# fc2's two upper products taken for both rows of a group together, in seven inner products each

## The chip, the cores and the metric

The kernel runs on one core of one Trainium2 chip, in one launch. The metric is the device time of that launch in microseconds (us). All arithmetic is float32; one matmul of a 128 x 128 weight tile with 256 columns appears in the profile as two records.

## The reference, cut to what matters

There are 16 rows b, each an x of 512 tokens by 512 features. A first layer computes h = gelu(x @ fc1.T + fc1_b), 2048 wide. A second layer, fc2, gives 384 shared outputs, and the row's own expert gives the last 128; so each row has its own 512 x 2048 weight matrix, of which three quarters are common to all rows. Then

```python
x = x + concat(h @ fc2.T + fc2_b, h @ experts_w[idx[b]].T + experts_b[idx[b]])      # x1
s = tanh(x @ W1 + b1) @ v                                 # one score per token
p = softmax(where(mask(prompt_type), s, -1e30))           # prefix, postfix or all but itself
x = x + (p @ x) / count
```

The last three lines are called pooling here. The kernel does them with a running maximum and linear recurrences along the tokens.

## The kernel before

The 16 rows go in 8 groups of two rows (`i`, `b0 = 2 * i`). A group has two stages on TensorE: fc1 for both rows at once, then fc2 for one row after the other.

Both layers use Strassen's scheme in Winograd's form: a product of 2 x 2 blocks takes seven block products and some sums. fc1 does so twice over: seven outer products, each of seven inner ones, 128 weight rows deep (`class Outer`, L555; its additions on VectorE are at L604, L618, L629, L645). fc2 does it once (`fc2`, L687): products 1 and 2 (banks `ba`, `bb`; weights `up`, blocks a11 and a12 of the upper half of the weights, which are the same for every row) and products 5, 7, 6, 3, 4 with the lower weights (`lo`) and the row's expert. Each of the seven is 16 matmuls of 256 columns (L724). The moving blocks b11, b12, b21, b22 are quarters of `hT`, the gelu of fc1; their sums (`t1` at L739, then L740, L744, L747) are VectorE's. `x1T` gets the result with the residual `xr` added (L764 to L775).

Weights come through a ring of ten 256 KB tiles, loaded on SyncE's queue in the order of `Ring.plan` and each waiting until the tile ten before it is free. fc1's inputs (`Moving`, tag `xT`) and the output stores use that queue too. PSUM has three banks `bx`, three `by` and one `bd`.

Each engine executes its instructions in the order in which the program issues them. Pooling is a Python generator per row (`class Pooling`, L834): a chain of some 40 small VectorE instructions on the scores (`weights`, L948), a store of the coefficients to DRAM and a load that spreads them over 128 partitions (L1078 to L1083) and ScalarE's copy of them (L1086), then per quarter of `x1T` a multiplication, a scan, two ScalarE passes, a multiplication and an addition (`apply`, L1092), and for most rows four transposes (L1193), each with its four stores (L1198). Every `yield` tells what a step costs VectorE in us by the author's estimate, or, if negative, asks for a pause. The estimates of one pooling add up to 24.15. While the matmuls of the other work are issued, `slot(budget, passed)` spends a small budget on the oldest unfinished pooling; the budgets stand in `SPARE` (fc1, 22.5 in a group's sum) and `SPARE_2` (fc2: 22.9 in a first row, 13.0 in a second). A row's pooling starts in the middle of the next stage: that of a first row in its group's second row, that of a second row in fc1 of the next group. Before a group's fc2 stands `drain(1)` (L1292), after its first row `drain()` (L1351):

```python
    def slot(budget, passed):                       # L1210
        while pools and pools[0].done:
            pools.pop(0)
        if pools:
            pools[0].slot(budget, passed)

    def drain(left=0):                              # L1216
        while len(pools) > left:
            slot(1e9, 1e9)
```

With a budget of 1e9 a pooling's own `slot` (L898) ignores pauses and goes to its end.

Of the kernel before, what the change touches and what calls it, by code (L numbers as in the profile page):

```python
# [9 lines left out]
F32 = mybir.dt.float32  # L10
I32 = mybir.dt.int32
AF = mybir.ActivationFunctionType
ALU = mybir.AluOpType
# [4 lines left out]
def tile_cond_experts_then_prompt_pool(  # L18
# [53 lines left out]
    LOWER = ("s1", "s3", "s2", "s4", "a22")  # L72


    WHERE = (
        (((0, 0), None, False),),
        (((1, 0), (0, 0), False),),
# [5 lines left out]
    )  # L83
    w1s = {
        (o, n): dram.tile([P, PW], F32, name=f"w1s_{o}_{n}") for o in OUTER for n in INNER if not (o in RAW and n in RAW)
    }
    w2s = {(n, h): dram.tile([P, PW], F32, name=f"w2s_{n}_{h}") for n in LOWER[:4] for h in range(2)}

# [4 lines left out]
    def piece1(o, n):  # L93
        (R, C), (r, c) = rc(o), rc(n)
        return fc1T[:, 2 * C + c, ds(R * (HID // 2) + r * PW, PW)]
# [68 lines left out]
    class Ring:  # L164
        def __init__(self):
            self.plan, self.tiles = [], {}
            for i in range(B // 2):
                b = 2 * i
                for o in OUTER:
                    self.plan += [("f1", i, o, p) for p in (INNER if i else INNER_0)]  # L170
                for r in range(2):
                    self.plan += [("up", b + r, "a11", h) for h in range(4)]
                    if not r:
                        self.plan += [("ex", b, "a11", h) for h in range(2)]
                    self.plan += [("up", b + r, "a12", h) for h in range(4)]
                    self.plan += [("ex", b + r, "a12", h) for h in range(2)]
                    self.plan += [("lo", b + r, n, h) for n in LOWER for h in range(2)]
                    if not r:
                        self.plan += [("ex", b + 1, "a11", h) for h in range(2)]
            self.at = 0  # L180
            self.taken, self.free = [], set()
# [14 lines left out]
        def pump(self):  # L196
            while self.at < len(self.plan) and self.room():
                key = self.plan[self.at]
                kind, b, n, h = key
                if kind == "lo" and n not in lower_done:  # L200
                    return
                if kind == "f1" and b == 0:
                    if not start_piece(n, h):
                        return
                else:
                    t = self.tiles[key] = self.tile(key)
                    if kind == "f1":
                        nc.sync.dma_start(t, w1s[n, h] if (n, h) in w1s else piece1(n, h))
                    elif kind == "up":
                        k = rc(n)[1] * KH + 2 * h  # L210
                        nc.sync.dma_start(as_chunks(t, 2), fc2T[:, k : k + 2, : 2 * P])
                    elif kind == "lo" and n in LOWER[:4]:
                        nc.sync.dma_start(t, w2s[n, h])
                    else:
                        nc.sync.dma_start(as_chunks(t), half2(n, 1 if kind == "ex" else 2, h))
                self.at += 1
# [202 lines left out]
            ring.pump()  # L419

    lower_done = {"a22"}

    ring = Ring()

# [262 lines left out]
    def fc2(b, hT, ex, at):  # L687
# [80 lines left out]
        at("3")  # L768
        add(out_block(0, 1), bc, u12, ALU.add)
        if b + 1 < B:  # L770
            xr_next[:] = [residual(b + 1, 0, 0), residual(b + 1, 1, 1)]
        if b + 1 < B:
            product(bd, of("a22"), b21, KH, "4", add=True)
            at("4")
# [47 lines left out]

        nc.scalar.activation(p1.tile([1, 1], F32, tag="c_none", name="none"), ones[0:1, :1], AF.Exp)
        return psc, x1T

# [388 lines left out]
# [3 lines that stand above are left out]
# [6 lines left out]
        "6m": 3.0, "6": 0.4, "3m": 3.0, "3": 2.5, "4m": 2.0,  # L1225
    }

    LAST_2 = {n + q: 1.7 for n in "57633" for q in ("a", "m", "c", "")}
    LAST_2.update({"6": 0.4, "3a": 0.8, "3m": 0.8})
    pool = xi_after = None  # L1230
    for i in range(B // 2):
# [9 lines left out]
        for n in range(7):  # L1241
            before, op = op, Outer(i, n, x, xi, hT)
            if i == 0:
                if n == 2:
                    nc.gpsimd.dma_start(w1_sb, w1)
                elif n == 4:
                    for h in range(2):
                        experts.load(h)
                    lower = Lower()
            for k in range(14):  # L1250
                if k % 2 == 0:
                    op.step(0, STEPS[k // 2])
                elif k >= LAG:
                    op.step(1, STEPS[(k - LAG) // 2])
                elif before:
                    before.step(1, STEPS[(k - LAG) // 2 + 7])
                tick()
                if n == 0 and i:
                    xi = xi_second
                elif n < 6:  # L1260
                    if k == 4:
                        x.outer_sum(n + 1, nc.gpsimd)
                    elif k == 7:
                        xi = x.inner_sums(n + 1, nc.gpsimd, (0, 1))
                    elif k == 10:
                        x.inner_sums(n + 1, nc.gpsimd, (2, 3))
                if i == 0:
                    if (n, k) == (2, 6):
                        start_outer("s4")
                    work()  # L1270
                    if n == 4:
                        lower.load()
                if pool and n == 0:
                    if k == 6:
                        pool.project()
                    elif k == 11:
                        pool.score()
                        pools.append(pool)

                if n or k >= 8:  # L1280
                    slot(SPARE[n], 0.86)
# [4 lines left out]
        if i == 0:  # L1286
# [3 lines left out]
            flush_stores()  # L1290
            xr_next[:] = [residual(0, 0, 0), residual(0, 1, 1)]
        drain(1)  # L1292
        for row in range(2):
            b = b0 + row
            more = row == 1 and b + 1 < B
# [2 lines left out]
            def at(name):  # L1298
                if b == 0:
                    for n in {"1a": ("s1",), "1c": ("s3",), "2m": ("s2",), "2": ("s4",)}.get(name, ()):  # L1300
                        lower.sums(n)
                    if name == "5":
                        fill()
                if row == 0:
                    if name == "1m":
                        for h in range(2):
                            experts.sum1(h)
                        for h in range(2):
                            experts.sums("a11", h)
                    elif name == "2m":  # L1310
                        for h in range(2):
                            experts.sums("a12", h)
                    elif name == "7":
                        nxt["ex"] = Expert(b + 1)
                        for h in range(2):
                            nxt["ex"].load(h)
                    elif name == "3m":
                        for h in range(2):
                            nxt["ex"].sum1(h)
                    elif name == "4m":  # L1320
                        for h in range(2):
                            nxt["ex"].sums("a11", h)
                else:
                    if name == "1a":
                        pool.project()
                    elif name == "1m":
                        pool.score()
                        pools.append(pool)
                    elif name == "2m":
                        for h in range(2):  # L1330
                            experts.sums("a12", h, nc.vector if b + 1 < B else nc.gpsimd)
                    if more and name == "2":
                        nxt["x"] = Moving(i + 1)
                    elif more and name == "7m":
                        nxt["xi"] = nxt["x"].inner_sums(0, nc.vector)
                        nxt["x"].outer_sum(1, nc.vector)
                    elif more and name == "6m":
                        nxt["xi_2"] = nxt["x"].inner_sums(1, nc.vector)
                if b + 1 == B:
                    if name == "1b":  # L1340
                        pool.rush()
                    elif name == "2":
                        before_last.flip_all("xT")
                    elif name == "end":
                        pool.flip_all("tx")
                    elif name in LAST_2:
                        slot(LAST_2[name], 1.7)
                elif name in SPARE_2 and not (row and name in ("3", "4m")):
                    slot(SPARE_2[name] * (0.4 if row and name in ("7m", "6m", "3m") else 1), 3.4)
                if b + 1 == B and name == "3":  # L1350
                    drain()  # L1351

# [53 lines left out]
```

## Time and profile before

| | us |
|---|---|
| time, median of 3 runs (1604.40 to 1608.44) | 1607.59 |
| time of the profiled execution | 1605.61 |
| its span | 1603.8 |
| TensorE busy in the span | 1564.2 |
| VectorE / ScalarE / GpSimd busy | 1160.1 / 621.2 / 393.3 |
| a group in the middle: fc1, 596.6 to 689.2 | 92.6 |
| the fc2 of both its rows, 689.2 to 789.6 and on to 790.5 | 101.3 |

In the profile PE is TensorE, PEld its weight loads, DVE VectorE, ACT ScalarE, POOL GpSimd and SP SyncE; "SPq" and "ACTq" are the issues of DMAs on those queues. A line of a timeline reads: start, duration, engine, line of the kernel, operation, what it writes and reads, how many, and in brackets how long the engine sat idle before it and what ended that. The profiled execution lies 1.98 us under the median, and 1.8 us of it lie outside the span.

### The profile page before, as it was taken

What the parts mean: (1) busy time and instruction counts of PE and PEld (TensorE: products, weight loads), DVE (VectorE), ACT (ScalarE), POOL (GpSimd) and SP (SyncE); (2) the same over time, 40 slices, a digit from 0 to 9 for tenths busy, and PEclk for the clock granted to TensorE, in tenths of its full rate; (3) what the DMA queues carried; (4) which work ended last, traced back from release to release, by engine and by line L of the source; (5) the groups of instructions that cost most, each with busy time, mean ns of one, the idle gap of its engine ahead of it and who ended that gap; (6) DMA issues with size and microseconds to landing.
All of it is one profiled execution on the core that took longest, in us unless ns stands there. A gap on an engine that the chain in (4) does not pass through costs nothing. (4 is left out here: it accounts for less than half of the span.)

```text
span 1603.8 us, 21941 instructions
## 1 busy us (share of the span) xinstructions
PE 1564.2 (98%) x6986; PEld 1317.9 (82%) x6986; DVE 1160.1 (72%) x2108; ACT 621.2 (39%) x1244; POOL 393.3 (25%) x426
## 2 busy tenths in 40 slices
PE   7999999999999999999999999999999999999995
PEld 6788878888788887888888887888878888788884
DVE  7875657967677676777678775887757967668676
ACT  2350145522453324633246223462244521454333
POOL 5541015200360004500045000630016200251020
PEclk9999999999999999999999999999999999999998
DMA  7667646658476574666656675576746658466542
GB/s 252 219 210 231 194 134 165 196 153 252 125 176 189 147 250 125 177 199 166 201 145 177 204 202 159 148 181 189 225 147 164 189 165 251 123 166 187 160 99 53
DMA packets 340094, 284.54 MB, mean 177 GB/s; under 512 B 145292, under 2 KB 264140, under 8 KB 339980
## 3 DMA queue, kind: packets, MB, share of 16 engines
q1 hardware_dynamic: 313580, 244.23, 53.3%
q0 software_dynamic: 5760, 19.97, 3.8%
q10 hardware_dynamic: 20640, 18.94, 3.8%
q8 instruction: 56, 0.92, 0.2%
q14 instruction: 58, 0.48, 0.1%
HBM read 253.55 MB, written 29.45 MB: 176 GB/s over the span
## 5 line engine op out<-in xcount | busy, mean ns | idle before, releaser
L591 ACT ACTIVATE hT<-hT,fc1b_sb 128x256 f32<-128x256 f32 x416 | 179.7, 498 | 64.7 <-DVE hT L645 49.4
L632 POOL TENSOR_TENSOR q<-p,hT 128x512 f32<-128x512 f32 x80 | 106.1, 1327 | 371.7 <-ACT p L625 360.1
L574 PE MATMUL bx<-xi,w_f_s_s 128*128 128x256 f32 x512 | 128.8, 384 | 3.8 <-DVE by L629 2.0
L724 PE MATMUL ba<-hT,w_up_a 128*128 128x256 f32 x512 | 116.7, 381 | 0.0
L724 PEld LDWEIGHTS ba<-hT,w_up_a 128*128 128x128 f32 x512 | 96.5, 190 | 23.1 <-issue 10.7
L574 PEld LDWEIGHTS bx<-xi,w_f_s_s 128*128 128x128 f32 x512 | 96.5, 191 | 22.1 <-DVE ba L618 5.3
L724 PE MATMUL bb<-hT,w_up_a 128*128 128x256 f32 x512 | 113.1, 379 | 0.0
L724 PE MATMUL bd<-hT,e 128*128 128x256 f32 x496 | 112.1, 379 | 0.0
L724 PEld LDWEIGHTS bb<-hT,w_up_a 128*128 128x128 f32 x512 | 97.3, 190 | 13.2
L724 PEld LDWEIGHTS bd<-hT,e 128*128 128x128 f32 x496 | 94.2, 190 | 12.8
L464 POOL DMA_INDIRECT e<-in_expT,rows x32 | 34.6, 1082 | 279.8 <-PE bd L724 241.7
L604 DVE TENSOR_TENSOR hT<-bx,hT 128x512 f32<-128x512 f32 x112 | 75.3, 684 | 32.1 <-PE bx L574 31.9
L574 PE MATMUL bx<-xi,w_f_a_s 128*128 128x256 f32 x384 | 95.9, 383 | 0.7 <-DVE by L629 0.4
L625 ACT COPY p<-bd 128x512 f32<-128x512 f32 x112 | 65.5, 585 | 79.8 <-PE bd L574 78.0
L1086 ACT COPY cb<-cb 128x1024 f32<-128x1024 f32 x15 | 15.7, 1045 | 204.8 <-DMA cb<-co_d 106.6
L629 DVE TENSOR_TENSOR by<-bx,p 128x512 f32<-128x512 f32 x112 | 77.5, 692 | 24.1 <-PE bx L574 23.6
L1151 ACT ACTIVATE v<-f,U,cb 128x512 f32<-128x512 f32 x60 | 48.9, 815 | 108.7 <-DVE U L1126 103.4
L1125 DVE TENSOR_TENSOR_SCAN f<-cb,u 128x512 f32<-128x512 f32 x60 | 79.6, 1326 | 12.9 <-ACT u L1117 12.2
L680 ACT ACTIVATE xr<-xr,fc2b_sb 128x256 f32<-128x256 f32 x96 | 44.9, 500 | 108.4 <-DVE p1x L743 39.2
L1133 DVE TENSOR_TENSOR f<-v,cb 128x512 f32 x60 | 45.9, 765 | 54.0 <-ACT v L1152 53.8
L1193 DVE STREAM_TRANSPOSE yo<-x1T 128x512 f32<-128x512 f32 x60 | 41.2, 701 | 59.2 <-DMA out_y<-yo 56.7
L574 PEld LDWEIGHTS bx<-xi,w_f_a_s 128*128 128x128 f32 x384 | 73.1, 191 | 12.1 <-issue 1.3
(292 smaller groups left out, 3492.7 us busy)
## 6 DMA issues: line engine op xcount, KB each, us to landing
w_up_a<-in_fc2T SPq DMA_DIRECT2D x128, 256.0 KB
w_lo_s<-w2s_s SPq DMA_DIRECT2D x128, 256.0 KB
w_f_s_s<-w1s_s_s SPq DMA_DIRECT2D x112, 256.0 KB
w_f_a_s<-w1s_a_s SPq DMA_DIRECT2D x84, 256.0 KB
w_f_s_a<-w1s_s_a SPq DMA_DIRECT2D x84, 256.0 KB
w_f_a_a<-in_fc1T SPq DMA_DIRECT2D x69, 256.0 KB
w_ex_a<-in_fc2T SPq DMA_DIRECT2D x64, 256.0 KB
xr<-in_xT ACTq DMA_DIRECT2D x64, 256.0 KB
```

What stands on the lines that cost most here:

```text
L574: nc.tensor.matmul(to.rearrange("p (b s) -> p b s", b=2) if len(mv.shape) == 3 else to, w[:, ts(2 * mh + m, P)], mv, start=(not add and m ...
L591: nc.scalar.activation(to[:, m], src[:, m], AF.Gelu, bias=fc1b_sb[:, hc + m : hc + m + 1])
L604: eng.tensor_tensor(to, src, self.place(prev, r, c, mh)[1], ALU.add)
L625: nc.scalar.copy(u["p5"], bd)
L629: add(u["y"], u["x"], u["p5"], ALU.add)
L632: nc.gpsimd.tensor_tensor(self.both(u["q"]), self.both(u["p5"]), self.place(self.to[0][1], 1, 1, mh)[1], ALU.add)
L680: nc.scalar.activation(t[:, m, :], t[:, m, :], AF.Identity, bias=bias)
L724: nc.tensor.matmul(bank[:, m, :], w(m, k), mv[:, k, :], start=(not add and m == 0 and k == 0), stop=(k == depth - 1), skip_group_check=True,)
L1125: V.tensor_tensor_scan(f[dc], c0, turned(u[dc]), 0.0, ALU.mult, ALU.add)
L1133: V.tensor_tensor(f[dc], turned(v[dc]), beta, ALU.mult)
L1151: nc.scalar.activation(v[dc][:, :S], f[dc], AF.Identity, bias=U[:, dc : dc + 1], scale=fac)
L1193: nc.vector.transpose(yo, self.x1T[:, dc, :])
```

## The change

In groups 1 to 6 (`joint`) products 1 and 2 of fc2 are taken for both rows together, each as seven inner products, in the order 1, 5, 6, 2, 7, 3, 4. One inner product is 4 matmuls, of 128 columns of each row. The sums of weights that this needs are made once, in group 0 (`UpperSums`), and kept in DRAM (`w2u`). The sums of `h` are GpSimd's, eight of 128 x 1024 in a group; the banks are combined by VectorE and ScalarE. Products 5, 7, 6, 3, 4 of each row follow (`Joint.row`). The pooling budgets of these groups are new (`JOINT_0`, `JOINT_1`, and four slots of 1.0 in `at_upper`), and add up to 16.9 before the end of the first row and 6.3 in the second. The load of the next group's `xT` is issued in product 5 of the second row; since the new sums lie in the buffer `xT`, it waits for the last read of them, the ScalarE copy behind that product. In group 0, one slot of the second row moves from "3m" to "4a". The diff, cut:

```diff
+    UPPER = ("a11", "s1", "s2", "a12", "s3", "s4", "a22")
+    UP_STEPS = (1, 5, 6, 2, 7, 3, 4)
+    def joint(i):
+        return 0 < i < B // 2 - 1
...
+                if joint(i):          # Ring.plan
+                    u = [("u2", b, o, n) for o in ("a11", "a12") for n in UPPER]
+                    self.plan += u[:4] + ex(0, "a11") + u[4:10] + ex(0, "a12") + u[10:] + lo(0, LOWER)
+                    self.plan += ex(1, "a11") + lo(1, LOWER[:1]) + ex(1, "a12") + lo(1, LOWER[1:])
+                    continue
...
+    class UpperSums:
+        def __init__(self):
+            self.t = p1.tile([P, 8, PW], F32, tag="xT", name="st_upper")
+        def load(self, o):
+            for k, n in enumerate(BLOCKS):
+                nc.scalar.dma_start(as_chunks(self.t[:, k]), half2(o, *rc(n)))
+        def sums(self, o, n):
...
+            nc.vector.tensor_tensor(to, self.t[:, at[in0]], self.t[:, at[in1]], op)
+            nc.gpsimd.dma_start(w2u[o, n], to)
...
+    class Joint:
+        def __init__(self, b0, hT):
+            self.t = p1.tile([P, 4, KH // 2, 2, Q], F32, tag="xT", name=f"th_{b0}")
+            self.o11 = self.t[:, 3]...
+        def sum(self, o, k, eng=nc.gpsimd):
...
+            eng.tensor_tensor(T(k), in0, in1, ALU.subtract)
+        def upper(self, xr, at):
...
+                for p in UP_STEPS:
+                    if p == 1:
+                        u["a"] = bank("by", f"ua_{b0}_{o}")
+                        product(x, 1)
+                        if one:
+                            nc.scalar.copy(u["a"][:, 0, :], x[:, 0, :])
+                        else:
+                            V.tensor_tensor(rows(u["a"]), rows(x), o11(0, 0), ALU.add)
+                    elif p == 5:
+                        product(bp, 5)
+                        nc.scalar.copy(u["p5"][:, 0, :], bp[:, 0, :])
+                        if one:
+                            self.sum("a12", 0)
+                    elif p == 6:
+                        product(x, 6, add=True)
+                        V.tensor_tensor(u["y"][:, 0, :], x[:, 0, :], u["p5"][:, 0, :], ALU.add)
...
+                        self.sum(o, 3)
+                    elif p == 2:
+                        product(u["a"], 2, add=True)
...
+                    elif p == 7:
+                        product(x, 7, add=True)
...
+                    at(f"u{tick}")
...
+        def row(self, r, ba, ex, xr, at, xr_after):
+            bc, bd = (bank("by", f"{n}2_{b}") for n in ("bc", "bd"))
+            product(bc, "s1", self.t1, "5")
+            nc.scalar.copy(out_block(0, 0), self.o11[:, r])
...
+    JOINT_0 = {"5m": 1.0, "5": 2.0, "7m": 1.0, "7": 2.0, "6m": 2.5, "6": 0.4, "3a": 1.0, "3m": 1.0, "3": 2.0}
+    JOINT_1 = {"5": 1.0, "7m": 0.6, "7": 2.5, "6m": 0.6, "6": 0.4, "4a": 1.2}
...
         drain(1)
+        if joint(i):
+            joined.sum("a11", 2)
+            def at_upper(name):
+                if name == "u1":
+                    joined.outer(0, 0)        # t1 of the first row, VectorE
...
+                if name in ("u8", "u9", "u11", "u12"):
+                    slot(1.0, 1.7)
...
+            ba = joined.upper([t() for t in xr_next], at_upper)
+            for r in range(2):
+                x1T = joined.row(...)
+                if r == 0:
+                    experts = nxt["ex"]
+                    drain()
+                before_last, pool = pool, Pooling(b0 + r, x1T)
+            continue
...
+                        nxt["up"] = UpperSums()          # group 0, first row, at "5"
+                        nxt["up"].load("a11")
...
-                elif name in SPARE_2 and not (row and name in ("3", "4m")):
-                    slot(SPARE_2[name] * (0.4 if row and name in ("7m", "6m", "3m") else 1), 3.4)
+                elif row and name == "4a":
+                    slot(SPARE_2["3m"] * 0.4, 5.1)
+                elif name in SPARE_2 and not (row and name in ("3m", "3", "4m")):
+                    slot(SPARE_2[name] * (0.4 if row and name in ("7m", "6m") else 1), 3.4)
```

## The prediction

> **What bounds the kernel now.** I read the page's first part, the waits of TensorE, then the timelines of one group. TensorE is the bound.
>
> ```profile
> PE 1564.2 (98%) x6986; PEld 1317.9 (82%) x6986; DVE 1160.1 (72%) x2108; ACT 621.2 (39%) x1244; POOL 393.3 (25%) x426
> ```
>
> In the middle groups it waits for almost nothing. The largest wait there is at the start of fc1, for the single bank `bd` that product 3 of fc2 has just filled; in the list of waits (total us, times, longest):
>
> ```profile
> PE bd L574 <- DVE x1T L769: 3.5, 3, 1.5
> ```
>
> In TensorE's timeline fc2's products 1 and 2 follow fc1 at once, and start 6.90 us apart: 16 matmuls, so 0.431 us each. The third line is the one long wait near the end: after 2.64 us of idling, 8 matmuls (16 records) took 5.41 us, 1.8 us more than the 3.62 of such a line elsewhere.
>
> ```profile
> 689.24 7.07 PE L724 MATMUL ba<-hT,w_up_a 128*128 128x256 f32 x32
> 696.14 7.07 PE L724 MATMUL bb<-hT,w_up_a 128*128 128x256 f32 x32
> ...
> 1558.40 5.41 PE L805 MATMUL bd<-hT,w_lo_a 128*128 128x256 f32 x16 [2.64 <-DVE p L756]
> ```
>
> So matmuls taken away count in full, as long as no other engine is made late. That is where the change has to be examined.
>
> **What it takes away.** Products 1 and 2 of two rows are 64 matmuls of 256 columns; in seven inner products they are 2 x 7 x 4 = 56. Six groups save 48 x 0.431 = 20.7 us. The banks `bc` and `bd` of fc2 are now both `by`, so fc1 no longer waits for L769: 3.5 us more.
>
> **What moves: the drain ahead of fc2.** The decisive point stands in the order of the changed program, which is fixed when it is built. A first row's pooling gets 6.3 of budget in the second row (13.0 before), then fc1's 22.5, less what the pauses waste. Before, its last transpose is issued within outer product 5 of fc1. In the changed order of groups 2 to 7 all four of its transposes come behind fc1's last addition: `drain(1)` finds this pooling unfinished. The loop then runs until one pooling is left in the list. But a finished pooling is taken from the list only by the next call of `slot`, and that call, with a budget of 1e9, goes on to drive the second one to its end. So VectorE's order reads: last addition of fc1, four transposes of row b0-2, the whole pooling of row b0-1, and only then `outer(0, 0)` and the addition `u["y"]` that inner product 7 waits for. ScalarE has the same: that pooling's passes stand ahead of the copy of inner product 1, which product 6 waits for. On SyncE the stores of eight transposes and the coefficients' round trip stand ahead of the ring loads that follow. TensorE can run 2 x 1.73 = 3.5 us before it needs ScalarE, and 4 x 1.73 = 6.9 us before it needs VectorE.
>
> The length of this burst, from the end of fc1's last matmul (689.24 in the group shown):
>
> First, the last addition of fc1 ends 0.9 after it. Then the transposes of row b0-2. Their buffer `yo` has two places, but one holds the next row's scores, so each waits for the store of the one before: starts 4.75 apart here, 4.75 to 5.45 in other groups (some are held by other work between); 4.9 taken. With no scores in the way the four took 7.3 (743.52 to 750.82).
>
> ```profile
> 664.22 0.71 DVE L1193 STREAM_TRANSPOSE yo<-x1T 128x512 f32<-128x512 f32 x1 [1.72 <-DMA out_y<-yo]
> 668.97 0.71 DVE L1193 STREAM_TRANSPOSE yo<-x1T 128x512 f32<-128x512 f32 x1 [0.60 <-DMA out_y<-yo]
> 689.44 0.69 DVE L604 TENSOR_TENSOR hT<-bx,hT 128x512 f32<-128x512 f32 x1
> 743.52 1.30 DVE L1193 STREAM_TRANSPOSE yo<-x1T 128x512 f32<-128x512 f32 x2 [0.40 <-POOL x1T L1177]
> 747.98 0.71 DVE L1193 STREAM_TRANSPOSE yo<-x1T 128x512 f32<-128x512 f32 x1 [3.15 <-DMA out_y<-yo]
> 750.11 0.71 DVE L1193 STREAM_TRANSPOSE yo<-x1T 128x512 f32<-128x512 f32 x1 [1.42 <-DMA out_y<-yo]
> ```
>
> 3 x 4.9 + 0.7 = 15.4: done at 16.3. Then the chain on the scores. The last group of the kernel before runs it without pauses for row 14, in 9.0 between these two lines and 0.2 for the instruction ahead: done at 25.5.
>
> ```profile
> 1521.57 0.22 DVE L970 SCALAR_TENSOR_TENSOR s<-s,is,s 32x16 f32<-32x16 f32 x1 [1.05 <-DMA s<-srow]
> ...
> 1530.38 0.20 DVE L1071 TENSOR_SCALAR sc<-q,is 32x1 f32<-32x1 f32 x1
> ```
>
> Then the round trip through DRAM and ScalarE's copy. From the end of L1071 to L1114 it took 10.4 here, and 8.6 to 10.0 in other rows; 9.3 taken, since the ring is full while TensorE stands: 34.8.
>
> ```profile
> 708.25 0.20 DVE L1071 TENSOR_SCALAR sc<-q,is 32x1 f32<-32x1 f32 x1
> 709.95 0.37 SPq L1083 DMA_DIRECT2D cb<-co_d  x1
> 717.77 1.04 ACT L1086 COPY cb<-cb 128x1024 f32<-128x1024 f32 x1 [17.54 <-DMA xr<-in_xT]
> 718.85 0.69 DVE L1114 TENSOR_TENSOR u<-x1T,cb 128x512 f32<-128x512 f32 x1 [1.10 <-ACT cb L1086]
> ```
>
> Then `apply`. From its first instruction to its first scan 1.5 (718.85 to 720.33), from scan to scan 4.31 where little stands between, and from the last scan to the end of the last addition 4.4 (1510.20 to 1514.59): 1.5 + 3 x 4.31 + 4.4 = 18.8, done at 53.6.
>
> ```profile
> 1499.66 1.22 DVE L1125 TENSOR_TENSOR_SCAN f<-cb,u 128x512 f32<-128x512 f32 x1
> ...
> 1503.97 1.22 DVE L1125 TENSOR_TENSOR_SCAN f<-cb,u 128x512 f32<-128x512 f32 x1
> ```
>
> GpSimd's correction (0.4) and the four transposes, now with two places (7.3): 61.3. `outer(0, 0)` is L739's 2.3, the addition of 128 x 256 0.4 (L808): 64.0. Inner product 7 would have started at 6.9, so TensorE stands 57.1, and by the row of 1558.40 loses 1.8 at the restart: 58.9 in each of groups 2 to 6, in all 294.5.
>
> Group 7 keeps the old fc2, but has the same drain: row 13 has no transposes, so the burst ends at 53.6. VectorE then has the expert's sums (2 x 0.64 + 4 x 0.6 = 3.7) and `t1` (2.3): 59.6. Product 5 needs `t1`, and products 1 and 2 cover 13.8: 45.8 + 1.8 = 47.6.
>
> **What it adds besides.** In group 1, without a burst, product 6 waits for ScalarE's copy of product 1 behind fc1's last gelus, which end at 4.3 in the group shown (1.7 without its two table loads of 1.28), the four residual passes (0.45 each) and the copy itself (0.45): 4.0 to 6.5 against 3.5, so 0.5 to 3.1; 2 taken. In the other groups the burst hides it. GpSimd's sums of 128 x 1024 have no row: 2 x 1.33 (L632) to 4 x 0.98 (`xi`) = 2.7 to 3.9; each has over 3.5 us of other inner products ahead of its use, or the burst, and is costed at nothing. VectorE's additional 1.7 us a group (smaller pieces, 0.25 to 0.7 each) fall into slots that have nothing left to do. The sums of weights in group 0 (8 x 0.68 on VectorE, loads on ScalarE's queue, stores on GpSimd's) lie where VectorE idles for TensorE (6.1 ahead of L756 in a row); uncovered, 5.5 at most. The later load of `xT` leaves some 28 us to fc1, for 2 MB: nothing, with 3 a group at most. SyncE's ring loads held behind the stores find ten tiles loaded, eight of them inner products' 1.73 us each: nothing to 5 a burst. The slot moved in group 0 costs nothing.
>
> The two engines can also collide. Beside a GpSimd addition, a VectorE multiplication took 1.53 instead of 0.68:
>
> ```profile
> 1545.33 2.05 POOL L1141 TENSOR_TENSOR x1T<-x1T,f 128x512 f32<-128x512 f32 x1 [8.64 <-DVE f L1133]
> 1546.40 1.53 DVE L1114 TENSOR_TENSOR u<-x1T,cb 128x512 f32<-128x512 f32 x1
> ```
>
> By this row the one GpSimd sum that can meet `outer(0, 0)` costs 0.85 in five groups: 4, kept for the range. The Trainium skill, page "SBUF — State Buffer", section "Who interferes with whom", speaks against the new sums more strongly: a VectorE instruction with two SBUF inputs is locked out for the whole of a GpSimd one. By that the same meeting would cost up to 2.7, or 13 in all; the row shows less, and the sum goes by the row.
>
> **The sum.** -20.7 - 3.5 + 294.5 + 47.6 + 2 = +319.9. On the profiled 1605.6 that is 1925.5; the median of the runs is 2.0 higher: 1927.5, or 1928.
>
> **The rivals.** *The drain stops after the first pooling* (the code would have to drop it at once): only the transposes remain, 16.3 + 2.3 + 0.4 = 19.0 against 6.9, 13.9 with the restart, five times, and 16.3 + 6.0 against 13.8, 10.3, in group 7. 79.8 - 24.2 + 2 = +58: 1665. The order of the program speaks against it. *Faster: the burst is hidden.* It would have to be under 6.9 us, for nothing else in TensorE's order lies between; then 24.2 are gained, six times 2 lost to ScalarE's copy: 1595. Only a VectorE that had run far ahead could do this, and it waits for fc1's last matmul. *A shorter burst*, where the first transposes go at the pace of the second (7.3 for 15.4): six times 8.1 less, 1879.
>
> **How the numbers follow.** The whole pooling in the burst, at any length: 0.92; the drain stopping early 0.04; hidden 0.03; something else 0.01. The range runs from the shorter burst, 1879, up by 1.5 (transposes) + 1.1 (round trip) + 1.1 (chain, 10.3 with its wait) + 1.2 (`apply`, if its last figures stretch) + 1.5 (restart) a burst, six times 6.4 = 38: 1966. A measurement can tell some 0.3% from no change. Faster 0.03, same 0.01, slower 0.96.
>
> **What would show it.** Right: TensorE idle for 50 us or more at the start of fc2 in groups 2 to 7, ended by VectorE's `u["y"]` (group 7: `t1`), none in group 1; TensorE's records down by 96; eight transposes in a row there. Wrong: the gaps missing or ending behind the first four transposes.

## The result, and the profile after

The changed kernel takes 1920.78 us (median of 4 runs, 1920.18 to 1921.75) against 1607.05 for the kernel before (4 runs): 1.196 times as long, 95% interval 1.195 to 1.198. Its profiled execution took 1920.44, with a span of 1918.6 us.

First the page's first part. TensorE has 96 records fewer, as the 48 matmuls taken away should make it, but its busy time has not fallen, and its share of the span went from 98% to 82%:

```profile
PE 1569.6 (82%) x6890; PEld 1316.7 (69%) x6890; DVE 1235.0 (64%) x2152; ACT 624.2 (33%) x1304; POOL 540.4 (28%) x488
```

Then TensorE's waits (what waited and for whom: us in total, times, longest). The first two lines together hold five stalls of about 46 us, those of groups 2 to 6, and the third is group 7's. The line for `bd` and L769 that stood here before is gone.

```profile
PE ux_a L908 <- POOL x1T L1388: 183.8, 4, 46.2
PE ux_a L908 <- issue: 77.5, 13, 45.8
PE bc L765 <- DVE t L780: 41.6, 1, 41.6
```

TensorE's timeline at the start of fc2 in group 3. Products 1 and 5 follow fc1 at once; product 6 starts 46 us late. The start after it is slow: 3.75 us for 8 records where such a line normally takes 1.89. There are two later, smaller gaps.

```profile
749.08 1.89 PE L908 MATMUL ux_a<-hT,w_u_a_a 128*128 128x256 f32 x8
750.80 1.89 PE L908 MATMUL up_a<-th,w_u_a_s 128*128 128x256 f32 x8
798.69 3.75 PE L908 MATMUL ux_a<-th,w_u_a_s 128*128 128x256 f32 x8 [45.99 <-POOL x1T L1388]
802.24 3.07 PE L908 MATMUL ua_a<-hT,w_u_a_a 128*128 128x256 f32 x8
808.38 3.47 PE L908 MATMUL ux_a<-th,w_u_a_s 128*128 128x256 f32 x8 [3.08 <-issue]
...
820.69 2.80 PE L908 MATMUL ux_a<-th,w_u_a_s 128*128 128x256 f32 x8 [1.94 <-issue]
```

VectorE's timeline over the same stretch says what was done meanwhile: fc1's last addition, four transposes each waiting for the store of the one before, row b0-1's chain on the scores (763.55 to 772.77), the round trip through DRAM (to 779.29), `apply` (to 798.2), four transposes more, and only then `outer(0, 0)` and `u["y"]`.

```profile
749.28 0.69 DVE L645 TENSOR_TENSOR hT<-bx,hT 128x512 f32<-128x512 f32 x1 [0.43 <-PE bx L615]
749.89 0.70 DVE L1404 STREAM_TRANSPOSE yo<-x1T 128x512 f32<-128x512 f32 x1
754.38 0.71 DVE L1404 STREAM_TRANSPOSE yo<-x1T 128x512 f32<-128x512 f32 x1 [3.79 <-DMA out_y<-yo]
...
763.55 0.18 DVE L1180 TENSOR_SCALAR s<-s,not 32x16 f32<-32x16 f32 x1
772.57 0.20 DVE L1282 TENSOR_SCALAR sc<-q,is 32x1 f32<-32x1 f32 x1
779.29 0.69 DVE L1325 TENSOR_TENSOR u<-x1T,cb 128x512 f32<-128x512 f32 x1 [6.53 <-ACT cb L1297]
...
797.48 0.69 DVE L1354 TENSOR_TENSOR x1T<-x1T,f 128x512 f32<-128x512 f32 x1
798.56 1.30 DVE L1404 STREAM_TRANSPOSE yo<-x1T 128x512 f32<-128x512 f32 x2 [0.40 <-POOL x1T L1388]
...
805.68 2.25 DVE L986 TENSOR_TENSOR t<-hT 128x2048 f32<-128x2048 f32 x1
807.85 0.43 DVE L940 TENSOR_TENSOR uy_a<-ux_a,up_a 128x256 f32<-128x256 f32 x1
```

The wait of 45.99 is put down to GpSimd's correction, the event that came last by the profile. Product 6 cannot use that; what it adds onto is the bank that ScalarE's copy of product 1 empties, and that copy ran at 798.23, behind the pooling's passes on ScalarE. ScalarE's timeline:

```profile
796.10 0.62 ACT L1363 COPY v<-v 128x512 f32<-128x512 f32 x1
796.62 1.70 ACT L721 ACTIVATE xr<-xr,fc2b_sb 128x256 f32<-128x256 f32 x4
798.23 0.36 ACT L927 COPY ua_a<-ux_a 128x256 f32<-128x256 f32 x1
```

So this gap is ended by ScalarE, and the next one, 3.08, by `u["y"]`. In the run after_dve below, where GpSimd has less to do, the list of waits names that copy itself:

```profile
PE ux_a L908 <- ACT ua_a L927: 231.9, 6, 46.2
```

### The profile page after: what moved, and what is told of

Its sections match the earlier page's. It is cut to its first block, busy times and chain, and to the rows that moved or that the text cites. A ratio compares the mean times of both kernels' runs of the same rounds, so it can differ in the third digit from the quotient of the medians.

```text
span 1918.6 us, 22137 instructions
## 1 busy us (share of the span) xinstructions
PE 1569.6 (82%) x6890; PEld 1316.7 (69%) x6890; DVE 1235.0 (64%) x2152; ACT 624.2 (33%) x1304; POOL 540.4 (28%) x488
## 5 line engine op out<-in xcount | busy, mean ns | idle before, releaser
L908 PE MATMUL ux_a<-th,w_u_a_s 128*128 128x256 f32 x192 | 64.0, 492 | 260.2 <-POOL x1T L1388 183.8
L908 PEld LDWEIGHTS ux_a<-th,w_u_a_s 128*128 128x128 f32 x192 | 45.8, 247 | 274.1 <-POOL x1T L1388 185.3
L670 DVE TENSOR_TENSOR by<-bx,p 128x512 f32<-128x512 f32 x112 | 77.6, 693 | 40.9 <-PE bx L615 40.9
L1344 DVE TENSOR_TENSOR f<-v,cb 128x512 f32 x60 | 63.3, 1055 | 49.8 <-ACT v L1363 49.8
L1003 PE MATMUL bd<-hT,e 128*128 128x256 f32 x384 | 86.8, 379 | 0.0
L1325 DVE TENSOR_TENSOR u<-x1T,cb 128x512 f32<-128x512 f32 x60 | 55.1, 919 | 39.5 <-ACT cb L1297 39.5
L1003 PEld LDWEIGHTS bd<-hT,e 128*128 128x128 f32 x384 | 73.0, 190 | 9.9
L645 DVE TENSOR_TENSOR hT<-by,hT 128x512 f32<-128x512 f32 x112 | 75.1, 682 | 4.2 <-PE by L615 1.3
```

The costliest lines, as they stand in the source:

```text
L645: eng.tensor_tensor(to, src, self.place(prev, r, c, mh)[1], ALU.add)
L670: add(u["y"], u["x"], u["p5"], ALU.add)
L908: nc.tensor.matmul(rows(bank), as_chunks(w)[:, k, :], moving[p][:, k], start=(not add and k == 0), stop=(k == KH // 2 - 1), skip_group_che ...
L1003: nc.tensor.matmul(bank[:, m, :], ex.of(n)[:, k, :] if m else as_chunks(lo[k // 4])[:, k % 4, :], mv[:, k, :], start=(not add and m == 0 a ...
L1325: V.tensor_tensor(u[dc][:, :S], x1T[:, dc, :], c1, ALU.mult)
L1344: V.tensor_tensor(f[dc], turned(v[dc]), beta, ALU.mult)
```

## The experiments

All times are medians, beside 1604 to 1606 for the kernel before, measured together with them. The table gives the lengths of three stages on TensorE in one group in the middle, group 4 (groups are counted from 0), from each run's timeline. Groups 2, 3, 5 and 6 differ from it by up to 3 us.

| us | fc1 | upper products | the rest of both rows | group |
|---|---|---|---|---|
| without joint products (no_joint) | 90.7 | 101.3 for all of fc2 | | 192.0 |
| the changed kernel | 91.8 | 81.2 | 73.7 | 246.6 |
| sums on VectorE (after_dve) | 89.8 | 82.0 | 73.7 | 245.4 |
| drain_one | 91.8 | 37.1 | 82.8 | 211.7 |
| budget | 102.5 | 31.4 | 76.1 | 210.1 |
| slots | 102.6 | 31.3 | 77.6 | 211.5 |
| slots_dve | 97.0 | 27.6 | 78.4 | 203.0 |
| late_dve | 95.8 | 27.6 | 85.1 | 208.4 |
| late_yo | 95.0 | 27.6 | 95.8 | 218.4 |
| overlap | 96.9 | 25.4 | 76.4 | 198.6 |
| shift | 103.5 | 25.4 | 76.5 | 205.4 |

The theory: the drain ahead of fc2 finds the pooling of row b0-2 unfinished, and runs it and the next one in one burst. The rivals: the joint products cost this by themselves, or the new sums on GpSimd do.

**The burst without joint products (before_low).** The kernel before, with only the smaller budgets for the slots of a second row:

```diff
+    LOW_2 = {"5": 1.0, "7m": 0.6, "7": 2.5, "6m": 0.6, "6": 0.4, "4a": 1.2}
+                elif row and i:
+                    slot(LOW_2.get(name, 0.0), 1.7)
```

> The kernel before, with its old products, whose second rows from group 1 on get the changed kernel's smaller pooling budgets (6.3 in all). In its program order the drain ahead of fc2 then holds four transposes and a whole pooling in groups 2 to 7, as in the changed kernel. If the burst is the cause: fc2's product 5 waits for t1. VectorE came to its sum ahead of fc2 56.6 us after fc1's end in the changed kernel; here 3.7 for the expert's sums and 2.3 for t1 follow, and products 1 and 2 cover 13.8, so 48.8 and 1.8 for the restart in five groups, and 41.6 + 1.8 in group 7: +296, some 1903 us (1880 to 1925). If the joint products are the cause: 1600 to 1615 us.

Measured: 1899.89, ratio 1.184 (1.181 to 1.188). No product is changed here, and 296 of the changed kernel's 314 us of loss are there. In its list of waits the stall has moved to product 5, and another name stands behind it: SyncE issues the load of that product's weights behind the drain's stores. In group 3 that load set the start, at 799.89; VectorE's `t1` was ready at 797.80, so the two queues end within 2.1 us of each other.

```profile
PE bc L724 <- DMA w_lo_s<-w2s_s: 251.5, 5, 50.6
```

**The joint products without the burst's second half (drain_one).**

```diff
-        while len(pools) > left:
+        while sum(not p.done for p in pools) > left:
```

> The changed kernel, whose drain counts only unfinished poolings, so that it stops behind the first one's four transposes. If the second pooling in the burst is the cause: the gaps ahead of inner product 6 or 7 shrink from 46 to some 10 us in groups 2 to 6, and to 7 in group 7; with the restarts +69, less 24 saved, and with 3 to 6 us of VectorE's waits for GpSimd's sums in each of six groups 1650 to 1700 us. If the joint products or the transposes are the cause: over 1850 us.

Measured: 1725.85, ratio 1.076 (1.073 to 1.079), 26 us above the range that I gave. The gaps at the start of fc2 are of the length worked out, but groups 2 to 6 have a second one, at the scores, that I had not expected. TensorE's timeline, the two gaps of group 3:

```profile
736.37 2.05 PE L908 MATMUL ux_a<-th,w_u_a_s 128*128 128x256 f32 x4 [9.52 <-issue]
804.34 1.86 PE L1071 MATMUL psc<-aT,v_sb 128*1 128x512 f32 x2 [5.97 <-ACT aT L1066]
```

The pooling that is no longer run in the burst is run later, at the `drain()` behind row 0, and ScalarE takes its passes ahead of the next row's tanh (L1066).

**A second place for the transposes (yo_two).**

```diff
+                yo = p1.tile([P, S], F32, tag="aT", ...) if dc % 2 and self.b % 2 == 0 else ...
```

> The changed kernel, whose transposes of first rows alternate between two buffers, so that each waits for the store before the last one. The burst stays, with 7.3 us instead of 13.7 for its first four transposes: six times 6.4 less, some 1882 us. If something else than VectorE's queue ends the gap (a DMA, GpSimd), the time stays at 1921.

Measured: 1883.32, ratio 1.174 (1.170 to 1.178). The transposes of row b0-2 take 7.2 us in place of 13.7, and TensorE's gap is 39.1 in place of 46.0 in group 3. A queue that is 6.5 us shorter makes a gap that is 6.9 us shorter.

**Budgets large enough (budget).** Of the changed kernel, only

```diff
+    JOINT_1 = {"5": 2.5, "7a": 1.5, "7m": 1.5, "7": 2.5, "6m": 1.2, "6": 0.4, "3m": 1.2, "4a": 2.2}
```

> The changed kernel with 13.0 instead of 6.3 of pooling budget in the second row of groups 1 to 6, so that the first row's pooling ends within fc1 and the drain finds nothing to do. If the burst is the cause, nothing over 5 us is left at the start of fc2. With the forecast's small terms (24.2 saved, 2 lost a group) 1595 us; if every group loses what group 1 lost in the changed kernel, where there is no burst (3.9 + 0.8 + 1.1 + 2.6 + 1.1 us), six times 9.5 against 24.2: 1640 us. If the joint products stall by themselves: over 1850 us.

Measured: 1713.46, ratio 1.068 (1.065 to 1.071). No burst is left, but the time is 73 us above the upper end of what I allowed for. The largest wait has moved to the start of fc1: there ScalarE's queue has the pooling's copy, which waits for the round trip, and four passes of `apply` ahead of fc1's copy of `ba` (L661, at 847.44).

```profile
841.46 1.04 ACT L1297 COPY cb<-cb 128x1024 f32<-128x1024 f32 x1 [11.99 <-DMA cb<-co_d]
848.06 1.22 PE L615 MATMUL bx<-xi,w_f_a_s 128*128 128x256 f32 x2 [6.53 <-ACT ba L661]
```

**The slots of fc1, and who makes the sums (slots, slots_dve).** The first has larger budgets in fc1 and in row 0, the second also has `eng=nc.vector` in `Joint.sum`:

```diff
+    SPARE = (0.7, 0.5, 0.5, 0.4, 0.4, 0.4, 0.4)
+    JOINT_0 = {"5m": 1.0, "5": 2.0, "7m": 1.5, "7": 2.5, "6m": 2.5, "6": 0.4, "3a": 2.0, "3m": 2.0, "3c": 2.0, "3": 2.5, "4a": 2.0, "4m": 2.0, "4c": 2.0}
+                    slot(1.5, 1.7)          # in at_upper
```

> Only budgets of the slots are changed, in fc1 (0.3 to 0.5, 0.0 to 0.4, 0.25 to 0.4) and in the joint stage, not in row 1, so that row b0-2's pooling ends inside fc1 and the drain ahead of the joint products finds one pooling and runs nothing. Burst theory with full port lock-out: the gap of 46 us and the two behind it (58 a group) go, and what is left of the loss are the 7 to 9 us a group that VectorE loses beside GpSimd's sums of 128x1024, against 48 x 0.431 = 20.7 saved: 1605 - 24 + 6 x 8 = about 1630, in 1600 to 1660. Rival, that the slots alone cannot hold the pooling (the 1713 of the wider budgets in row 1 is then the price of two poolings in less room): 1680 to 1720 again, with waits for ScalarE's copies in fc1.

> The run before it with one more edit: the 24 sums of hT into the joint products' operands on VectorE, not on GpSimd. If VectorE is locked out while GpSimd adds 128x1024 tiles: the waits for hT at the end of fc1 and in the first upper products shrink to 1 or 2 us a group, and the time falls by 25 to 50 us, to 1585 to 1610. If the lock-out costs little where it lies: same within 10 us, or slower, by VectorE's 24 x about 1.2 = 29 us of work at the turn.

Measured: 1702.13 (1.059, 1.057 to 1.061) and 1660.76 (1.034, 1.032 to 1.036). The first misses the burst theory's 1630: fc1 becomes 11.9 us longer than without joint products. The second is 41 us faster than the first, a fall of the size expected, but it too misses its range, 1585 to 1610, because it starts from 1702. It shows how much of the first one's loss is GpSimd's sums: these 41 us, 5.6 of fc1's 11.9 a group among them. In TensorE's timeline of the first, the wait at the end of fc1:

```profile
720.81 1.22 PE L615 MATMUL bx<-xi,w_f_a_a 128*128 128x256 f32 x2 [4.52 <-DVE hT L686]
```

**No joint products (no_joint).**

```diff
-        return 0 < i < B // 2 - 1       # joint(i)
+        return False
```

> joint(i) is false for every group, so no joint product is taken; what is left of the change are group 0's slot and the unused definitions. Every theory: as before, 1604 to 1609.

Measured: 1600.90 (10 runs), ratio 0.997 (0.996 to 0.998): some 4 us faster than the kernel before, where I expected no difference. What remains of the change is the slot of each second row that moved from inside product 3 to product 4 ("4a"), in every group here, and the eight sums of weights that group 0 still makes. In its profile the waits for `bd` and L769, 3.5 us in the kernel before, are no longer among TensorE's largest. This is the fastest kernel of the study.

**The sums on VectorE, with the burst (after_dve).** Of the changed kernel, only

```diff
-        def sum(self, o, k, eng=nc.gpsimd):
+        def sum(self, o, k, eng=nc.vector):
```

> The changed kernel with one edit: its 24 sums of hT for the joint products on VectorE, not on GpSimd. The burst stays (six groups, about 50 us each). Lock-out theory: what goes are the waits that come of VectorE standing still beside a GpSimd sum, some 7 us in group 1 and in groups 2 to 7 the 1.9 us ahead of the burst and part of the second gap of 3 to 5 us, while VectorE gains 24 x 1.2 us of work, a third of it on the path: 1920 less 15 to 40, about 1890. Rival, that the sums cost nothing beside the burst: 1915 to 1925.

Measured: 1919.05, ratio 1.196 (1.193 to 1.199): the rival's time. fc1 is 2.0 us a group shorter, the upper products 0.8 longer, in which the sums now stand in VectorE's queue with the burst. So in the changed kernel the choice of engine hardly matters; with the budgets of the run slots, where there is no burst, it is worth 41 us.

**Three more ways to place the pooling (late_dve, late_yo, overlap).** All have the sums on VectorE and `drain_one`'s loop. In late_dve the drain comes behind the upper products, fc1's fourth budget is 0.2, and both rows have more slots. late_yo also lets transposes take turns between `yo` and `aT`.

```diff
-        drain(1)
+        if not joint(i):
+            drain(1)
...
             ba = joined.upper([t() for t in xr_next], at_upper)
+            drain(1)
+    SPARE = (0.6, 0.3, 0.3, 0.2, 0.25, 0.25, 0.25)
+    JOINT_0 = {"5a": 1.0, "5m": 1.0, ... "3": 2.5, "4a": 2.0, "4m": 2.0, "4c": 2.0}
```

> Sums on VectorE, the drain moved from ahead of the joint products to behind them and stopping once one pooling is left unfinished, fc1's fourth slot budget 0.2 and not 0.0, three slots of row 1 somewhat larger, more slots in row 0. So fc1 keeps nearly the budgets of the kernel before (the slots run gave them up, and its fc1 took 97 to 103 us a group where the kernel without joint products took 90.7). If the crowding of fc1 was the price there: fc1 back to 91 to 93 us, 1610 to 1640, about 1625. If VectorE's work in the joint stage is what binds (row 0's drain still runs half a pooling): 1640 to 1665, no better than the slots run with the sums on VectorE. Below 1600 if all waits go and only 20.7 saved is left.

> As late_dve, and the transposes of a pooling take turns between the tile yo and the tile aT, so that the drain behind row 0 doesn't wait for each store: 3 to 8 us a group off the waits at the end of row 0 where they are on the path, 1600 to 1630; the same as late_dve within 5 us if they are not.

Measured: 1696.86 (1.059, 1.056 to 1.061) and 1749.61 (1.092, 1.090 to 1.094). Both miss. In late_dve TensorE waits 9 us in each of groups 2 to 6 for the addition L1033, the last of row 0: slots inside product 4 had put steps of `apply` ahead of it on VectorE, where the expert's sums stand too. In late_yo the scores wait 8 us besides: `aT` has one place, and the next row's tanh, which writes it, waited behind the transposes (the last began at 812.25) and their stores; L986, which the bracket names, does not touch that tile. ScalarE's timeline:

```profile
816.67 0.69 ACT L1066 ACTIVATE aT<-pa,b_sb 128x512 f32<-128x512 f32 x1 [12.83 <-DVE hT L986]
```

For overlap the drain stands ahead of the joint products again, the slots inside product 4 were taken out, those before it in row 0 are larger, row 0's sum of b12 was moved out of the upper products, and a slot that finds the first pooling in a pause between transposes goes on with the second:

```diff
+        if len(pools) > 1 and pools[0].flipping and pools[0].pause > passed:
+            pools[0].pause -= passed
+            pools[1].slot(budget, passed)
+    SPARE = (0.6, 0.3, 0.3, 0.3, 0.25, 0.25, 0.25)
```

> Sums on VectorE; the drain stops once one pooling is unfinished; a slot that finds the first pooling only pausing between its transposes goes on with the second; fc1's budgets are those of the kernel before but for 0.3 in place of 0.0 at its fourth outer product; row 0's last steps (4a, 4m, 4c) have no slot, so that no transposes that wait for stores stand ahead of the additions which the pooling's projections need; VectorE's sum of b12 for row 0 is taken in row 0 and not among the upper products. If the two misses before came of those transposes (9 us a group) and of fc1's crowding (6 us a group): fc1 91 to 93 us, upper products 25 to 27, the two rows 74 to 76 a group, 190 to 196 against 192 in the kernel without joint products, so 1595 to 1625, most likely 1610. If VectorE has no room for the pooling beside the joint products wherever it is put: 1650 or more.

Measured: 1652.18, ratio 1.028 (1.025 to 1.031), outside 1595 to 1625 and within the rival's "1650 or more". The upper products (25.4) came out as expected; the rows did not quite (76.4 in group 4, 78.6 to 79.4 in groups 2, 3, 5 and 6, where 74 to 76 was expected), and fc1 (96.9) did not. In its trace TensorE waits 2.1 us a group, in the fifth outer product, for GpSimd's `xi`, whose sums are issued within the fourth, where the changed budget is used. The attribution in this expectation was wrong as well: what delayed L1033 in late_dve was `apply`, not transposes.

**The fourth budget back to 0.0 (shift).** The steps go to row 1 instead, and the projections and scores come 2 and 3.5 us later:

```diff
+    SPARE = (0.6, 0.3, 0.3, 0.0, 0.25, 0.25, 0.25)
+    JOINT_1 = {"5": 1.5, "7a": 0.8, "7m": 1.0, "7": 2.5, "6m": 1.0, "6": 0.4, "3m": 0.6, "4a": 1.2}
```

> As the overlap run, with two edits: fc1's fourth outer product has the budget 0.0 again, its 4.2 us of steps being put into row 1 (about 9 us of budget in place of 7.3, so that the pooling of row b0 comes into fc1 with its copy for ScalarE still 2 slots away); and the projections of a pooling stand 2 us later in row 1, its scores 3.5 us later. If the overlap run's fc1 (96.9 us a group against 90.7 without joint products) was long because of that fourth budget: fc1 91 to 94, the rows 74 to 75 us without the 2.5 us wait of the projections, 190 to 195 a group, and 1652 less 6 x 5 to 7 = 1610 to 1622, within 1 % of the kernel before and hardly faster. If VectorE is short of room over the whole group: the time only moves, 1640 to 1660.

Measured: 1693.21, ratio 1.055 (1.053 to 1.057). It missed because ScalarE's copy was not two slots away when fc1 began, but already issued: as in budget, it waits for the round trip in ScalarE's queue, ahead of fc1's first copy.

```profile
827.43 1.04 ACT L1299 COPY cb<-cb 128x1024 f32<-128x1024 f32 x1 [18.81 <-DMA cb<-co_d]
829.01 1.22 PE L615 MATMUL bx<-xi,w_f_a_s 128*128 128x256 f32 x2 [8.30 <-ACT ba L661]
```

The start of fc1 takes 11.1 us longer for it (15.5 to the projections in place of 4.4). Less that, fc1 is 92.4, which fits the fourth budget as the cause of most of what overlap's fc1 had too much (96.9 against 90.7); it was not changed alone. No version tried has both the poolings' steps in row 1 and the copy out of fc1's way, and none with joint products beats the kernel before. The rival, that VectorE has no room for the pooling beside the joint products wherever it is put, is not ruled out. Whether a faster version exists stays open.

## Why the prediction was right

**The matmuls taken away.** 96 records fewer, as predicted. What the 20.7 us would be worth without the burst was not reached: the best upper products took 25.4 us a group where 14 x 1.73 = 24.2 are left of the work, and the best rest of the rows 73.7, never both in one kernel. Together 99.1 against 101.3 for fc2 without joint products, so 2.2 of the 3.45 a group.

**The bank `bd`.** The 3.5 us did go, but the reason given was not shown. no_joint keeps the old banks and loses the same waits, with nothing of the change left but the moved slot and group 0's sums of weights. The prediction costed the moved slot at nothing.

**The burst.** This was the sum, and it was there in groups 2 to 7 and not in group 1. before_low shows that the budgets and the drain make it, without any joint product. Its terms in group 3, predicted and measured: first transposes from one to the end of the fourth 15.4 and 13.7; chain 9.2 and 9.2; round trip and copy 9.3 and 6.5; `apply` 18.8 and 18.9; second transposes 7.3 and 7.2. The upper products of groups 2 to 6 took 79.6, 82.0, 81.2, 80.4 and 80.1, so 282.3 over their 24.2, where 294.5 was predicted. The round trip and the pace of the stores are what was sized too long: both were taken from rows in which TensorE and the ring were working, and in the burst they stand still; that this is the reason was not tested by itself. Of the 282.3, the gaps in TensorE's timeline are 256.8, where 5 x 57.1 = 285.5 was predicted, and the rest, 25.5, is matmuls that run slowly after a gap, where 5 x 1.8 = 9 was predicted: the restart was sized by one slow line, and each burst has several. So here too two errors partly cancel.

The sign named in advance, 50 us or more of idling ended by `u["y"]`, holds only for the sum of a group's gaps (49.8 to 52.1 in groups 2 to 6). The long gap itself is 46 and ends with ScalarE's copy, a wait that the prediction names but does not put first. Group 7, whose gap does end with `t1`: 41.6 and a slow start of 5.28 in place of 3.62, 43.3 in all, 47.6 predicted.

**GpSimd's sums.** Costed at nothing, and within 2 us right for this kernel (after_dve), but by luck of the place. The row by which the collision was priced (1.53 for 0.68) was too small, because there the two instructions overlapped only in part. In group 1 of the changed kernel, GpSimd's and VectorE's timelines:

```profile
299.00 2.42 DVE L1219 TENSOR_SCALAR mm<-mm,ab 32x17 f32<-32x17 f32 x1
299.05 2.34 POOL L887 TENSOR_TENSOR th<-hT,th 128x1024 f32<-128x1024 f32 x1
301.36 2.34 POOL L887 TENSOR_TENSOR th<-hT 128x1024 f32<-128x1024 f32 x1
301.45 2.27 DVE L1223 TENSOR_TENSOR ex<-mm 32x16 f32<-32x16 f32 x1
...
305.06 1.13 PE L615 MATMUL bx<-xi,w_f_a_a 128*128 128x256 f32 x4 [3.87 <-DVE hT L686]
```

L1223 handles 32 x 16 numbers and lasts as long as the sum beside it. In after_dve, where GpSimd makes no such sum, the same two instructions of group 1 take 0.22 (L1219) and 0.16 (L1223). These two put the addition L686 off by more than 4 us, and TensorE waits 3.87. That is the rule the prediction had set aside: the Trainium skill, page "SBUF — State Buffer", section "Who interferes with whom", says that the loser is locked out for the whole of the other's instruction. Here the trace agrees with the page. Group 1 loses some 11 us where 2 was predicted (3.87 here, and 7.1 in its upper products, 31.3 for 24.2). Not all of that is shown to be GpSimd's: with the sums on VectorE (after_dve) fc1 and the upper products of group 1 together are only 4.1 us shorter, though VectorE then has the sums to make. And each fc1 before a burst is 1.1 longer than without joint products. A GpSimd sum of 128 x 1024 itself took 2.35, less than the 2.7 to 3.9 that bounded it.

**The sum.** -24.2 + 282.3 + 43.3 + 11 + 5 x 1.1 = 318, against 1918.6 - 1603.8 = 314.8 between the two spans. The prediction had 319.9: its five bursts were 12 us and group 7 4 us too long, and 9 us in group 1 and 5.5 in fc1 were missing from it, so its small error is partly due to errors that cancel, and that is luck. The sum of the measured terms is 3 us more than the spans show; where these lie was not traced.

**The rivals.** The drain that stops early, priced at 1665, takes 1726 when it is built: its gap was right and the price of doing the pooling later was missing. The shorter burst, priced at 1879, takes 1883.

## What to carry to other kernels

Before a stage is shortened, ask which background work lives in its slots: here a stage that gave up 3.5 us of TensorE's time a group also gave up VectorE's and ScalarE's slots, and what no longer fitted came back in one piece at the next drain, more than ten times as dear. Look at the order in which each engine issues its instructions, not at the sum of its busy time: a copy that waits for a DMA, a transpose that waits for a store or a small step that waits beside GpSimd's sum holds up everything queued behind it. And a loop that "runs until one is left" should say what counts as left.

## What the hardware showed unexpectedly

VectorE's small instructions stood still beside GpSimd's additions, down to 32 x 16 elements: 2.27 us where 0.16 is usual.

TensorE's slow starts go with the clock that the profile says was granted, as a share of full speed. In group 3 it was 0.50 from 756.8 to 804.6, 1.00 to 808.0, 0.50 to 811.4, and 0.50 again from 821.7 to 825.1; the slow lines shown above overlap the stretches of 0.50. How long TensorE had idled does not decide it alone: 8 records took 2.80 us after 1.94 us of idling there, but in group 1 of the same run 1.97 after 2.63 us, at a clock of 1.00. TensorE's timeline in group 1:

```profile
328.44 1.97 PE L908 MATMUL ux_a<-th,w_u_a_s 128*128 128x256 f32 x8 [2.63 <-issue]
```

In the whole run TensorE was busy for 67.3 us at a clock of 0.50, against 16.0 in the kernel before. At half the clock these 51 us hold about 26 us of work, by estimate; the other 26, less the 20.7 of the matmuls taken away, are the 5 us by which its busy time rose.
